# Graph layers on one core: the last stage recast with features on the partitions, node degrees taken in the pattern stage

## The chip, the core and the metric

The kernel runs on one NeuronCore of a Trainium2 chip. Such a core has TensorE (matmuls, with the weight load as its own instruction), VectorE, ScalarE and GpSimd (POOL in the profile), and SyncE (SP), which here only issues DMAs. Each engine executes its own list of instructions in order; semaphores tie them together. The metric is the device time of one execution in microseconds (us); before the change the median of three runs is 4073.85 us (4073.61 to 4083.79).

## The reference

Sixteen graphs of 1024 nodes with 128 features each pass through four layers; every layer is `x = layernorm(x + layer(x, adj))`. `adj` is symmetric in its pattern but not in its values, sparse (some eight neighbours a node), and never negative. Cut to what matters:

```python
# layer 0: attention over the neighbours
x = _layernorm(x + _L0(x, adj, ...))
# layer 1: thin the pattern row by row, then three graph convolutions
adj_d = adj * _dilate(adj > 0)
for l in 1, 2, 3:                      # h0 = x
    deg = clip(sum(adj_d, -1), 1)
    out = (adj_d @ h / deg) @ Wr + h @ Wx + b
    h_l = batchnorm(relu(out / norm(out)))
x = _layernorm(x + concat(h1, h2, h3) @ Wl + bl)
# layer 2
x = _layernorm(x + relu(adj @ (x @ W + b) + x))
# layer 3: A1 = adj + I, d = rsqrt(sum(A1, -1))
x = _layernorm(x + ((A1 * d[:, None] * d[None, :]) @ x) @ B)
```

After the thinning nearly every node keeps no edge but itself; the few others ("slots", at most 128 a graph) are handled apart. A general path, not executed for this data, stands behind a flag.

## The kernel before

The kernel is written for a tile framework: the code gives operations on tiles, and the framework orders each engine's instructions, by their place in the program and by when it reckons them ready, and sets the semaphores. So a queue's order is near the program's, but loads can stand earlier. Four stages follow one another; B is 16 graphs, T is 8 tiles of 128 nodes, N = 1024, F = P = 128.

**phase_att** (layer 0) is not touched. It leaves x1 in DRAM in two forms, `x1_d` (nodes by features) and `x1T_d` (features by nodes), and the 0/1 pattern `mask_d` in f16.

**phase_pattern** (layer 1's thinning) has a generator `find(b)` for each graph. It loads the 2 MB pattern `m` (L599, SP; three buffers), counts each row with eight ScalarE activations with a sum (L603), builds `md` on GpSimd (L607), settles which nodes are small with matmuls against `m` (L617, L621), numbers the remaining ones as slots (L644, L646), gathers their adjacency rows by an indirect DMA on GpSimd's queue (L664), multiplies the pattern with the slots' one-hot matrix (L673, after which `m` is free), turns the gathered rows with TensorE (L703), copies them with ScalarE (`turned`, L705) and multiplies again (L709). `rolling(tasks, depth, lag)` interleaves the generators: at most three graphs are open, and a graph is begun once the one before has made four steps. `settle` and `alone` finish the pattern.

**phase_conv** (the three convolutions) runs over 18 sets a layer: 16 graphs and two sets of slots. For a graph it takes `hT` (features by nodes; in layer 1 loaded from `x1T_d`, L914, later made from `uT` by batch norm's scale and shift, L910), multiplies it on GpSimd with a broadcast row `dd` (load L944, product L946), makes `pq` with 16 matmuls (L949, L950), adds the bias (L952), norms and rectifies to `u` (L954 to L964) and turns `u` into the SBUF tile `uT` one set later (`turn`, L896 to L901). In layers 2 and 3 each `hT` is written to `hT_d` (L912). At the end the slots' share of the output goes to `os_d` (L1009).

**phase_end** (the projection of layer 1, layers 2 and 3, three layer norms) works on one graph at a time, nodes on the partitions. `start(b)` loads the 4 MB transposed adjacency (`adj`, L1058, two buffers), x1 and the h's, and per tile of 128 nodes does four matmuls with h as the stationary side (L1081, L1082), adds, and takes row statistics; `layernorm_tail` (L65 to L69) computes 1/std with a GpSimd power (L67) and scales with eight VectorE operations. `layer2` turns x with TensorE (`turned`, L1048, L1049), makes `vals` = x W + b with a 129th column of ones (L1095, L1096), and for each of eight node tiles sums eight matmuls with a 128x128 piece of the adjacency stationary and 129 columns of `vals` moving (L1102); the extra column comes out as the node's degree (L1106), from which `d` follows (L1114). `layer3` does the same with `v3` = d (x W3) and 128 columns (L1123 to L1138) and writes y (L1140, L1141). The order in the program is

```python
    start(0)
    for b in range(B):
        layer2(b)
        if b + 1 < B:
            start(b + 1)
        layer3(b)
```

Of the kernel before, what the change touches and what calls it, by code (L numbers as in the profile page):

```python
# [10 lines left out]
F32 = mybir.dt.float32  # L11
# [11 lines left out]
P = 128  # L23
# [527 lines left out]
def phase_pattern(ctx, tc, t, c, mask_d, dd_d, slots_d, keep, flags):  # L551
# [44 lines left out]
    def find(b):  # L596
# [7 lines left out]
        yield  # L604
        md = wp.tile([P, T, P], F16, name="md", bufs=3)
        for ti in range(T):
            nc.gpsimd.tensor_tensor(md[:, ti, :], m[:, ti, ti * P : (ti + 1) * P], less, ALU.mult)  # L607
        s = sm.tile([P, T], F16, name="s")
# [16 lines left out]


# [6 lines left out]
        nc.vector.tensor_tensor(left[:, b, :], deg, pu, ALU.subtract)  # L633

# [16 lines left out]
        yield  # L651
        pc = ps_s.tile([P, P + 1], F32, name="pc", tag="ps")
# [15 lines left out]
        yield  # L668

# [17 lines left out]
        yield  # L687
        pr = ps_s.tile([P, P + 1], F32, name="pr", tag="ps")
# [8 lines left out]
        yield  # L697

# [7 lines left out]
        yield  # L706
        pv = ps_s.tile([P, P], F32, name="pv", tag="ps")
# [155 lines left out]
def phase_conv(ctx, tc, t, c, x1_d, x1T_d, dd_d, slots_d, keep, hT_d, uT, os_d):  # L863
# [17 lines left out]
    wl = cp.tile([P, 3, F], F32, name="wl")  # L881
    nc.sync.dma_start(wl, t["L1_gnn_Wl"].rearrange("(l p) f -> p l f", p=P))

    for layer in (1, 2, 3):
# [7 lines left out]
        def turn(s, u):  # L892
            for half in range(2):
# [6 lines left out]
                nc.scalar.copy(to, flat)  # L900
                nc.vector.bn_stats(stats[:, 2 * s + half, :], flat)  # L901

        late = None
        for s in range(SETS):
# [3 lines left out]
            if layer > 1:  # L908
                src = uS[:, layer - 2, (s - B) * N : (s - B + 1) * N] if slots else uT[:, s * N : (s + 1) * N]
                nc.scalar.activation(hT, src, AF.Identity, scale=bn[:, 0:1], bias=bn[:, 1:2])  # L910
                if not slots:
                    nc.sync.dma_start(hT_d[layer - 2][s], hT)  # L912
# [100 lines left out]
def phase_end(ctx, tc, t, c, x1_d, keep, hT_d, uT, os_d, ys, out):  # L1013
# [3 lines left out]
    ap = ctx.enter_context(tc.tile_pool(name="e_a", bufs=2))  # L1017
    wp = ctx.enter_context(tc.tile_pool(name="e_w", bufs=2))
    small = ctx.enter_context(tc.tile_pool(name="e_s", bufs=4))
    ps_p = ctx.enter_context(tc.tile_pool(name="e_pp", bufs=2, space=PSUM))  # L1020
    ps_g = ctx.enter_context(tc.tile_pool(name="e_pg", bufs=4, space=PSUM))
    ps_t = ctx.enter_context(tc.tile_pool(name="e_pt", bufs=2, space=PSUM))

    bn = keep.bn[2]
    node_row = cp.tile([P, N], F16, name="node_row")
    nc.sync.dma_start(node_row, t["q_node_row"])
    wl = cp.tile([P, 3, F], F32, name="wl")
    nc.sync.dma_start(wl, t["L1_gnn_Wl"].rearrange("(l p) f -> p l f", p=P))
    bl = cp.tile([P, F], F32, name="bl")
    nc.sync.dma_start(bl, row_broadcast(t["L1_gnn_bl"], F))  # L1030
# [6 lines left out]
    vals = []  # L1037
    for i in range(2):
        v = cp.tile([P, T, F + 1], F32, name=f"vals{i}")
        nc.vector.memset(v[:, :, F : F + 1], 1.0)  # L1040
        vals.append(v)

    def turned(x):
        xT = wp.tile([P, N], F32, name="xT")
        for half in range(2):
            pt = ps_t.tile([P, 4, P], F32, name="pt")
            for j in range(4):
                nc.tensor.transpose(pt[:, j, :], x[:, half * 4 + j, :], c.ident)  # L1048
            nc.scalar.copy(xT[:, half * 512 : half * 512 + 512], pt.rearrange("p t i -> p (t i)"))  # L1049
        return xT  # L1050

    S = {}

    def start(b):

        s = S[b] = Consts()
        s.adj = ap.tile([P, T, N], F32, name="adj")
        nc.sync.dma_start(s.adj, t["adjT"][b].rearrange("(t p) i -> p t i", p=P))  # L1058
        s.x = wp.tile([P, T, F], F32, name="x")
        nc.sync.dma_start(s.x, x1_d[b].rearrange("(t p) f -> p t f", p=P))  # L1060
        h = []
        for l in range(3):
            hT = wp.tile([P, N], F32, name=f"h{l}")
            if l < 2:
                nc.sync.dma_start(hT, hT_d[l][b])  # L1065
            else:
                nc.gpsimd.tensor_scalar(
                    hT, uT[:, b * N : (b + 1) * N], bn[:, 0:1], bn[:, 1:2], op0=ALU.mult, op1=ALU.add
                )
            h.append(hT)  # L1070

        to = wp.tile([P, N], F32, name="to", bufs=1)
        nc.gpsimd.tensor_scalar(to, node_row, keep.node[:, b : b + 1], None, op0=ALU.is_equal)
        end = wp.tile([P, F], F32, name="end")
        nc.sync.dma_start(end, os_d[:, b, :])
        mv = small.tile([P, T, 2], F32, name="mv")
        for it in range(T):
            at = slice(it * P, (it + 1) * P)
            pp = ps_p.tile([P, F], F32, name="pp")
            for l in range(3):  # L1080
                nc.tensor.matmul(pp, h[l][:, at], wl[:, l, :], start=l == 0, stop=False)  # L1081
            nc.tensor.matmul(pp, to[:, at], end, start=False, stop=True)  # L1082
            o = small.tile([P, F], F32, name="o", bufs=2)
            nc.vector.tensor_tensor(o, pp, bl, ALU.add)  # L1084
            nc.vector.tensor_tensor(s.x[:, it, :], o, s.x[:, it, :], ALU.add)  # L1085
            row_stats(nc, small, s.x[:, it, :], mv[:, it, :])
        layernorm_tail(nc, small, c, s.x, mv, s.x)

    def layer2(b):
        s = S[b]  # L1090
        xT = turned(s.x)
        v = vals[b % 2]
        for it in range(T):
            pp = ps_p.tile([P, F], F32, name="pp")
            nc.tensor.matmul(pp, xT[:, it * P : (it + 1) * P], w2, start=True, stop=True)  # L1095
# [737 lines left out]
```

## Time and profile before

| what | value | from |
|---|---|---|
| runs | 4083.79, 4073.85, 4073.61 us | the times |
| profiled execution | 4084.57 us, its span 4082.8 us | the profiled run |
| mean granted TensorE clock | 0.892 | the profiled run |
| phase_att | to about 2265 us | first load of the pattern stage |
| find() of the pattern stage | 2273 to 2640 us | L599 to L710 |
| settle, alone | 2640 to 2727 us | L750 to L849 |
| phase_conv | 2727 to 3226 us | L949 to L1009 |
| phase_end | 3226 to 4082.8 us | L1058 to the last output |
| L1102, layer 2's matmuls | 2048 instructions of 275 ns (median) | group by line |
| L1129, layer 3's matmuls | 2048 instructions of 275 ns (median) | group by line |
| DMA over the span | 341.32 MB, 84 GB/s | the page |

An f32 matmul of the program is two matmul instructions with a weight load each, here called passes, so that 1024 matmuls of L1102 are 2048 instructions. The duration of one is not its cost: matmuls overlap, and the distance between the starts counts. "Busy" is the share of time in which an engine has an instruction under way. "PEld" is TensorE's weight load, which runs beside the matmuls. The clock is what was granted to TensorE, as a part of full speed.

### The profile page before, as it was taken

The numbers are of one execution on the slowest core, as the hardware profiler recorded it, in microseconds if no ns is written. First come the engines' busy times: TensorE is split into PE (matmuls) and PEld (weight loads), VectorE is DVE, ScalarE is ACT, GpSimd is POOL, SyncE is SP. The second block draws the span as 40 slices with busy tenths as digits, with TensorE's granted clock in tenths as the row PEclk, the third lists the DMA queues.
The fourth block names the chain that finished last, engine by engine and source line by source line (L and its number), as shares of the span: only waits on it lengthen the run. The fifth ranks groups of instructions, "written<-read, shape, count | busy, mean of one in ns | idle before, by whom it ended". The sixth has DMA issues, their size and how long they took to land. (4 is left out here: it accounts for less than half of the span.)

```text
span 4082.8 us, 81190 instructions
## 1 busy us (share of the span) xinstructions
PE 3260.5 (80%) x30587; PEld 2820.9 (69%) x30587; DVE 2887.1 (71%) x10905; ACT 1216.5 (30%) x3329; POOL 1633.7 (40%) x2069
## 2 busy tenths in 40 slices
PE   4888888888888888888999565666667599999997
PEld 2776766676666666676777465646666588888887
DVE  3788888888878888788899445576556366666665
ACT  3433333333333333333333453302334200000000
POOL 9545554545454445545432221125546222222221
PEclk9999999999989999999999676778778799999999
DMA  5222122212212221222100342223323323333331
GB/s 144 80 65 68 47 66 71 65 48 68 65 55 57 70 65 48 65 68 65 33 22 12 132 151 88 70 88 118 116 80 127 143 104 125 125 124 125 124 113 41
DMA packets 146435, 341.32 MB, mean 84 GB/s; under 512 B 12848, under 2 KB 52272, under 8 KB 145904
## 3 DMA queue, kind: packets, MB, share of 16 engines
q1 hardware_dynamic: 135536, 301.41, 23.4%
q0 software_dynamic: 10496, 34.62, 2.5%
q8 instruction: 242, 3.96, 0.4%
q14 instruction: 161, 1.32, 0.1%
HBM read 258.32 MB, written 77.66 MB: 82 GB/s over the span
## 5 line engine op out<-in xcount | busy, mean ns | idle before, releaser
L384 PE MATMUL pg<-ch,oh 104*128 104x256 bf16 x4800 | 908.6, 286 | 120.9 <-ACT hg L395 116.8
L420 PE MATMUL pa<-hg,we 128*104 128x129 f32 x3200 | 672.4, 303 | 106.7 <-DVE we L417 99.0
L420 PEld LDWEIGHTS pa<-hg,we 128*104 128x104 f32 x3200 | 462.0, 179 | 264.2 <-DVE we L417 167.6
L386 PE MATMUL pg<-a,oh 104*128 104x128 bf16 x4800 | 590.0, 227 | 0.0
L417 DVE TENSOR_SCALAR we<-k_id,idc,e 128x104 f32<-128x104 f16 x1600 | 588.6, 386 | 0.0
L384 PEld LDWEIGHTS <-oh 104*128 104x128 bf16 x4800 | 430.1, 102 | 174.5 <-issue 125.6
L391 DVE SCALAR_TENSOR_TENSOR junk<-pg,w_a 128x128 f32<-128x128 f32 x1600 | 409.4, 285 | 166.8 <-PE pg L386 133.6
L234 POOL TENSOR_SCALAR mask<-ld 104x1024 f16<-104x1024 f32 x144 | 400.7, 2782 | 312.1 <-DVE one_way L336 170.8
L386 PEld LDWEIGHTS <-oh 104*128 104x128 bf16 x4800 | 427.2, 102 | 52.0
L395 ACT COPY hg<-pg 128x256 f32<-128x256 f32 x800 | 293.9, 372 | 405.9 <-DVE junk L391 396.2
L1102 PE MATMUL pg<-vals,adj 128*128 128x129 f32 x2048 | 262.1, 285 | 0.0
L237 ACT ACTIVATE neg<-ld 104x1024 bf16<-104x1024 f32 x144 | 152.2, 1057 | 348.5 <-DMA ld<-in_adjT 348.5
L1102 PEld LDWEIGHTS pg<-vals,adj 128*128 128x128 f32 x2048 | 255.2, 203 | 0.0
L1129 PE MATMUL pg<-v,adj 128*128 128x128 f32 x2048 | 240.2, 276 | 0.0
L1129 PEld LDWEIGHTS pg<-v,adj 128*128 128x128 f32 x2048 | 235.0, 192 | 0.0
L1049 ACT COPY xT<-pt 128x512 f32<-128x512 f32 x64 | 36.0, 587 | 657.0 <-PE pt L1048 657.0
L349 ACT CAST oh<-pw 104x512 bf16<-104x512 f32 (+3 forms) x288 | 138.0, 485 | 214.2 <-PE pw L346 213.6
L387 PE MATMUL ids<-k_id_col,oh 104*128 104x1 f16 x1600 | 179.4, 167 | 25.7 <-ACT idc L403 25.7
L311 DVE TENSOR_TENSOR g<-k_slot,off 105x1280 f16<-105x1280 f16 (+9 forms) x160 | 159.1, 994 | 52.1 <-ACT off L307 51.6
L949 PE MATMUL pq<-w,hT 128*128 128x128 f32 x768 | 168.1, 305 | 17.9 <-ACT hT L910 11.7
L285 PE MATMUL pw<-w_all,xT 128*104 128x512 f32 x320 | 182.2, 653 | 0.0
L964 DVE SCALAR_TENSOR_TENSOR u<-q,nrm 128x1024 f32<-128x1024 f32 x54 | 89.4, 1655 | 121.8 <-POOL nrm L962 121.8
(310 smaller groups left out, 7193.7 us busy)
## 6 DMA issues: line engine op xcount, KB each, us to landing
adj<-in_adjT SPq DMA_DIRECT2D x16, 4096.0 KB
ld<-in_adjT SPq DMA_DIRECT2D x144, 416.0 KB
m<-mask_d SPq DMA_DIRECT2D x16, 2048.0 KB
mask_d<-mask SPq DMA_DIRECT2D x144, 208.0 KB
dd<-dd_d SPq DMA_DIRECT2D x48, 512.0 KB
hT_d<-hT SPq DMA_DIRECT2D x32, 512.0 KB
h<-hT_d SPq DMA_DIRECT2D x32, 512.0 KB
xT<-in_xTp SPq DMA_DIRECT2D x16, 520.0 KB
```

The lines of the kernel that those rows point to most:

```text
L234: nc.gpsimd.tensor_scalar(mt[:W, s, :N], ld[:W], 0.0, None, op0=ALU.is_gt)
L285: nc.tensor.matmul(pw[:W], d.xT[:, i * W : (i + 1) * W], w_all, start=True, stop=True)
L384: nc.tensor.matmul(pg[:, n, :], other, d.ch[:W, j, p, :], start=p == 0, stop=False)
L386: nc.tensor.matmul(pg[:, n, :F], own, a3[:W, p, :], start=False, stop=p == 2)
L387: nc.tensor.matmul(ids[:, j : j + 1], own, k_id_col[:W], start=True, stop=True)
L391: nc.vector.scalar_tensor_tensor(junk, pg[:, n, :F], 0.0, w_a2, op0=ALU.max, op1=ALU.mult, accum_out=d.sc[:, at : at + 1],)
L395: nc.scalar.copy(hg[:, j0 : j0 + 2, :F], pg[:, :, F:])
L417: nc.vector.tensor_scalar(we[:, j, :], k_id, idc[:, j : j + 1], e[:, j : j + 1], op0=ALU.is_equal, op1=ALU.mult)
L420: nc.tensor.matmul(pa[:W], we[:, j, :], hg[:, j, :], start=j == 0, stop=j == NG - 1)
L949: nc.tensor.matmul(pq[:, it, :], hT[:, at], w[:, :F], start=True, stop=False)
L1102: nc.tensor.matmul(pg, s.adj[:, jt, it * P : (it + 1) * P], v[:, jt, :], start=jt == 0, stop=jt == T - 1)
L1129: nc.tensor.matmul(pg[:, :F], s.adj[:, jt, it * P : (it + 1) * P], v[:, jt, :], start=jt == 0, stop=jt == T - 1,)
```

## The change

The diff has three parts.

1. *Degrees in the pattern stage.* `find(b)` gets a helper `weights(ti)`: it loads 128 rows of the adjacency in f32 (512 KB, SP, four buffers) and sums them with a ScalarE activation into `keep.deg`. Its eight calls are spread over the steps of `find`. The column of ones in `vals` goes.
2. *phase_conv writes u instead of h.* `turn` writes each half of `uT` to `u_d` (three layers, two writes of 256 KB a graph); the writes of `hT_d` go. `uT` becomes a tile of this stage. The columns' means are taken out of `Wl`, so that layer 1's output needs no mean in its layer norm.
3. *phase_end is rewritten* as a generator `batch(b)` for each graph, two of them interleaved by `rolling(..., 2, 6)`; `adj` has three buffers. Batch norm is folded into `wl` and a constant; d for all graphs is computed at the start with 16 GpSimd powers. The projection and layer 2 run with features on the partitions: `wl` or `v2` stationary, 512 columns of u or of the adjacency moving. Layer norm 1 takes the variance with one-column matmuls against 1/F (`pv`) and spreads 1/std over the partitions with matmuls against the identity (`pr`). The result of layer 2 is turned to nodes on the partitions with TensorE (`pt`), and layer 3 then works as before with 128x128 pieces of the adjacency stationary. Scaling of layer norms 2 and 3 moves from VectorE to ScalarE.

```diff
             junk = wp.tile([P, N], BF16, name="junk")
             nc.scalar.activation(junk, m[:, ti, :], AF.Relu, accum_out=deg[:, ti : ti + 1])
         yield
+
+        def weights(ti):
+
+            a = wp.tile([P, N], F32, name="a_rows", bufs=4)
+            nc.sync.dma_start(a, t["adj"][b, ti * P : (ti + 1) * P, :])
+            junk = wp.tile([P, N], BF16, name="junk")
+            nc.scalar.activation(junk, a, AF.Relu, accum_out=keep.deg[:, b, ti : ti + 1])
+
         md = wp.tile([P, T, P], F16, name="md", bufs=3)
         for ti in range(T):
             nc.gpsimd.tensor_tensor(md[:, ti, :], m[:, ti, ti * P : (ti + 1) * P], less, ALU.mult)
+        weights(0)
         s = sm.tile([P, T], F16, name="s")
         nc.vector.tensor_scalar(s, deg, KEEP - 1.0, None, op0=ALU.is_le)
         yield
@@ -623,6 +632,7 @@
                 )
             return pu
...
+        weights(1)
...
-    wl = cp.tile([P, 3, F], F32, name="wl")
+    uT = cp.tile([P, B * N], F32, name="uT")
+    wl = keep.wl
     nc.sync.dma_start(wl, t["L1_gnn_Wl"].rearrange("(l p) f -> p l f", p=P))
+    mean = small.tile([P, 3], F32, name="mean_w")
+    nc.vector.tensor_reduce(mean, wl, AX.X, ALU.add)
+    nc.vector.tensor_scalar(mean, mean, 1.0 / F, None, op0=ALU.mult)
+    nc.vector.tensor_tensor(wl, wl, mean.unsqueeze(2).to_broadcast([P, 3, F]), ALU.subtract)
 
     for layer in (1, 2, 3):
...
                 nc.scalar.copy(to, flat)
+                if s < B:
+                    nc.sync.dma_start(u_d[layer - 1][s, :, half * 512 : half * 512 + 512], to)
                 nc.vector.bn_stats(stats[:, 2 * s + half, :], flat)
...
                 nc.scalar.activation(hT, src, AF.Identity, scale=bn[:, 0:1], bias=bn[:, 1:2])
-                if not slots:
-                    nc.sync.dma_start(hT_d[layer - 2][s], hT)
...
-def phase_end(ctx, tc, t, c, x1_d, keep, hT_d, uT, os_d, ys, out):
+def phase_end(ctx, tc, t, c, x1T_d, keep, u_d, os_d, ys, out):
...
+    share = cp.tile([P, P], F32, name="share")
+    nc.vector.memset(share, 1.0 / F)
+
+    pm = ps_s.tile([P, 4, P], F32, name="pm", tag="ps")
+    nc.tensor.matmul(pm[:, 0, :], share, w3, start=True, stop=True)
+    nc.vector.tensor_tensor(w3, w3, pm[:, 0, :], ALU.subtract)
+
...
+    for l in range(3):
+        nc.tensor.matmul(
+            pm[:, 1, :], keep.bn[l][:, 1:2].to_broadcast([P, P]), keep.wl[:, l, :],
+            start=l == 0, stop=l == 2,
+        )
+        nc.vector.tensor_scalar(wl[:, l, :], keep.wl[:, l, :], keep.bn[l][:, 0:1], None, op0=ALU.mult)
+    nc.vector.tensor_tensor(bl, bl, pm[:, 1, :], ALU.add)
+    nc.tensor.transpose(pm[:, 2, :], bl, c.ident)
+    const = cp.tile([P, 1], F32, name="const")
+    nc.vector.tensor_copy(const, pm[:, 2, 0:1])
+
+    d_all = cp.tile([P, B, T], F32, name="d_all")
+    nc.gpsimd.tensor_scalar(d_all, keep.deg, 1.0, None, op0=ALU.add)
+    for b in range(B):
+        nc.gpsimd.tensor_tensor(d_all[:, b, :], d_all[:, b, :], c.mhalf, ALU.pow)
+
+    def big(name):
+        return ps_b.tile([P, N], F32, name=name, tag="pb")
...
+    def norm(tiles, mv, name):
+
+        for it, z in enumerate(tiles):
+            row_stats(nc, small, z, mv[:, it, :])
+        ve = small.tile([P, T], F32, name=f"ve_{name}")
+        nc.gpsimd.tensor_tensor(ve, mv[:, :, 1], c.eps, ALU.add)
+        rs = small.tile([P, T], F32, name=f"rs_{name}")
+        nc.gpsimd.tensor_tensor(rs, ve, c.mhalf, ALU.pow)
+        off = small.tile([P, T], F32, name=f"off_{name}")
+        nc.vector.scalar_tensor_tensor(off, mv[:, :, 0], -1.0, rs, op0=ALU.mult, op1=ALU.mult)
+        return rs, off
...
+    def batch(b):
+        adj = ap.tile([P, T, N], F32, name="adj")
+        nc.sync.dma_start(adj, t["adjT"][b].rearrange("(t p) i -> p t i", p=P))
+        x = wide("x1")
+        nc.sync.dma_start(x, x1T_d[b])
+        u = []
+        for l in range(3):
+            w = wide(f"u{l}")
+            nc.sync.dma_start(w, u_d[l][b])
+            u.append(w)
+        end = wp.tile([P, F], F32, name="end")
+        nc.sync.dma_start(end, os_d[:, b, :])
+
+        to = wide("to")
+        nc.gpsimd.tensor_scalar(to, node_row, keep.node[:, b : b + 1], None, op0=ALU.is_equal)
+        yield
+
+        pz = big("pz")
+        for l in range(4):
+            for h in (slice(0, 512), slice(512, N)):
+                nc.tensor.matmul(
+                    pz[:, h], wl[:, l, :] if l < 3 else end, u[l][:, h] if l < 3 else to[:, h],
+                    start=l == 0, stop=l == 3,
+                )
+        z = wide("z1")
+        nc.vector.scalar_tensor_tensor(z, pz, const, x, op0=ALU.add, op1=ALU.add)
+        sq = wp.tile([P, N], F32, name="sq", tag="to")
+        nc.scalar.activation(sq, z, AF.Square)
+        yield
+        pv = ps_s.tile([P, 4, P], F32, name="pv", tag="ps")
+        for it in range(T):
+            nc.tensor.matmul(
+                pv[:, 0, it : it + 1], sq[:, it * P : (it + 1) * P], share[:, 0:1], start=True, stop=True
+            )
+        ve = small.tile([P, T], F32, name="ve")
+        nc.vector.tensor_scalar(ve, pv[:, 0, :T], LN_EPS, None, op0=ALU.add)
+        rs = small.tile([P, T], F32, name="rs")
+        nc.gpsimd.tensor_tensor(rs, ve, c.mhalf, ALU.pow)
+        yield
+        pr = big("pr")
+        for it in range(T):
+            nc.tensor.matmul(
+                pr[:, it * P : (it + 1) * P], rs[:, it : it + 1].to_broadcast([P, P]), c.ident,
+                start=True, stop=True,
+            )
+        x2 = wide("x2")
+        nc.vector.tensor_tensor(x2, z, pr, ALU.mult)
+        yield
+
+        v = rows("v2")
+        for k, ph in enumerate(halves("ph")):
+            for j in range(4):
+                at = (k * 4 + j) * P
+                nc.tensor.matmul(ph[:, j, :], x2[:, at : at + P], w2, start=True, stop=True)
+            nc.vector.tensor_tensor(
+                v[:, k * 4 : k * 4 + 4, :], ph, b2.unsqueeze(1).to_broadcast([P, 4, F]), ALU.add
+            )
+        yield
+        pg = big("pg")
+        for m in range(T):
+            for h in (slice(0, 512), slice(512, N)):
+                nc.tensor.matmul(pg[:, h], v[:, m, :], adj[:, m, h], start=m == 0, stop=m == T - 1)
+            if m == 3:
+                yield
+        z2 = wide("z2")
+        nc.vector.tensor_tensor(z2, pg, x2, ALU.add)
+        nc.vector.scalar_tensor_tensor(z2, z2, 0.0, x2, op0=ALU.max, op1=ALU.add)
+        yield
+        pt = halves("pt")
+        for it in range(T):
+            nc.tensor.transpose(pt[it // 4][:, it % 4, :], z2[:, it * P : (it + 1) * P], c.ident)
+        mv = small.tile([P, T, 2], F32, name="mv2")
+        rs, off = norm([pt[it // 4][:, it % 4, :] for it in range(T)], mv, "2")
+        d = d_all[:, b, :]
+        scale = small.tile([P, T], F32, name="scale")
+        nc.gpsimd.tensor_tensor(scale, rs, d, ALU.mult)
+        x3 = rows("x3")
+        for it in range(T):
+            nc.scalar.activation(
+                x3[:, it, :], pt[it // 4][:, it % 4, :], AF.Identity,
+                scale=rs[:, it : it + 1], bias=off[:, it : it + 1],
+            )
+        yield
+
+        v = rows("v3")
+        for k, pw in enumerate(halves("pw")):
+            for j in range(4):
+                it = k * 4 + j
+                nc.tensor.matmul(pw[:, j, :], z2[:, it * P : (it + 1) * P], w3, start=True, stop=True)
+                nc.scalar.activation(v[:, it, :], pw[:, j, :], AF.Copy, scale=scale[:, it : it + 1])
+        yield
+        mv = small.tile([P, T, 2], F32, name="mv3")
+        for k in range(2):
+            pg = ps_s.tile([P, 4, P], F32, name="pg3", tag="ps")
+            for j in range(4):
+                it = k * 4 + j
+                for m in range(T):
+                    nc.tensor.matmul(
+                        pg[:, j, :], adj[:, m, it * P : (it + 1) * P], v[:, m, :],
+                        start=m == 0, stop=m == T - 1,
+                    )
+                if j == 1:
+                    yield
+            o = small.tile([P, 4, F], F32, name="o", bufs=1)
+            nc.vector.tensor_tensor(o, pg, v[:, k * 4 : k * 4 + 4, :], ALU.add)
+            for j in range(4):
+                it = k * 4 + j
+                nc.vector.scalar_tensor_tensor(
+                    x3[:, it, :], o[:, j, :], d[:, it : it + 1], x3[:, it, :], op0=ALU.mult, op1=ALU.add
+                )
+            yield
+        rs, off = norm([x3[:, it, :] for it in range(T)], mv, "3")
+        y = ys[b % 2]
+        for it in range(T):
+            nc.scalar.activation(
+                y[:, it, :], x3[:, it, :], AF.Identity, scale=rs[:, it : it + 1], bias=off[:, it : it + 1]
+            )
+        nc.gpsimd.dma_start(out[b].rearrange("(t p) f -> p t f", p=P), y)
+        yield
+
+    rolling([(b, batch(b), []) for b in range(B)], 2, 6)
...
+        keep.deg = lp.tile([P, B, T], F32, name="keep_deg")
+        keep.wl = lp.tile([P, 3, F], F32, name="keep_wl")
         ys = [lp.tile([P, T, F], F32, name=f"y{i}") for i in range(2)]
```

## The prediction

> **What bounds the kernel now.** I read the page first, then busy time by stretch, then the chain of waits and the timeline of one batch, and last the two queues that get new work (ScalarE's and SP's).
>
> ```profile
> span 4082.8 us, 81190 instructions
> PE 3260.5 (80%) x30587; PEld 2820.9 (69%) x30587; DVE 2887.1 (71%) x10905; ACT 1216.5 (30%) x3329; POOL 1633.7 (40%) x2069
> ```
>
> The attention stage, which the change leaves alone, ends at about 2265 us. The other stages, cut at their first and last instructions (columns: stretch, length, busy time of five engines, granted clock, DMA share, GB/s):
>
> ```profile
> core 0: us, PE busy (x) PEld busy (x) DVE busy (x) ACT busy (x) POOL busy (x), PEclk, DMA share, GB/s
> 2273.00:2640.00 367.00, 223.97 (x3652) 215.44 (x3652) 166.00 (x428) 174.88 (x337) 74.83 (x144) 0.71 0.34 118
> 2727.00:3226.00 499.00, 340.85 (x2368) 326.14 (x2368) 288.71 (x299) 174.35 (x221) 247.81 (x225) 0.81 0.33 106
> 3226.00:3268.00 42.00, 17.08 (x100) 16.13 (x101) 11.89 (x47) 1.17 (x2) 11.09 (x7) 0.60 0.84 312
> 3268.00:4046.00 778.00, 709.15 (x5635) 679.90 (x5634) 502.31 (x2076) 74.85 (x180) 177.08 (x147) 0.94 0.32 115
> ```
>
> The rows are find(), phase_conv, the end stage's first loads, and its steady part. Find is bound by no engine: none is over 61% busy. The steady end stage is TensorE's: 91% busy. The chain of waits gives its period, 51.2 us a batch, as the distance of these two rows:
>
> ```profile
> 3514.18 1.66 POOL rstd L67
> ...
> 3565.39 1.66 POOL rstd L67
> ```
>
> The timeline says what one batch spends. Each f32 matmul is two passes.
>
> ```profile
> 3499.77 12.72 PE L1129 MATMUL pg<-v,adj 128*128 128x128 f32 x112
> 3518.26 0.49 PE L1095 MATMUL pp<-w,xT 128*128 128x128 f32 x2 [2.35 <-DVE vals L1096]
> 3520.03 0.64 PE L1095 MATMUL pp<-w,xT 128*128 128x128 f32 x2
> 3539.03 2.27 PE L1048 MATMUL pt<-ident,x 128*128 128x128 f32 x8 [1.65 <-DVE x L69]
> 1000.33 1.08 PE L285 MATMUL pw<-w_all,xT 128*104 128x512 f32 x2
> ```
>
> 112 passes of 128 columns in 12.72 us, the last lasting 0.28: 0.112 us a pass. A batch has 64 (L1081, L1082), 16 transposes, 16, 128, 16 and 128 passes: 368 x 0.112 = 41.2 us. The other 10 us are stalls (2.35 and 1.65 us above) and the half-rate passes after them (a pair starts every 0.43 us at 3520, twice the 0.22 of a full-speed pair). The last row, from the attention stage, prices a 512-column pass: two take 1.08 us and one lasts 0.653 (L285's mean), so they start 0.427 us apart.
>
> **The change, part by part: the end stage.** Moving 512 columns streams the same columns through the array. Four narrow passes cost 4 x 0.112 = 0.448 us, one wide pass 0.427. Layer 2's aggregation goes from 128 passes (14.3 us) to 32 (13.7); the head projection from 64 (7.2) to 16 (6.8). Layer 3's aggregation keeps the adjacency stationary, 128 narrow passes, 14.3: the label does not hold there. Of 16 transposes 8 stay (0.9). New are pr (16 passes, 1.8) and pv (16 one-column passes; not shown in f32, between the 0.03 of L617's f16 rows and 0.112: 0.5 to 1.8, I take 1.8). ph and pw stay at 1.8 each. Sum 6.8 + 1.8 + 1.8 + 1.8 + 13.7 + 0.9 + 1.8 + 14.3 = 42.9 us against 41.2. So TensorE gets no less work; only the 10 lost us can be won.
>
> [...]
>
> What can be lost again: in a batch, between the end of pg and a full-rate pg3, lie z2 (two 128x1024 VectorE operations, 1.22 each as at L952 and L964, with hand-overs 2.8), the first transposes 0.5, eight pairs of statistics at 0.45 (3.6), ve, rs and scale on POOL (0.2 + 1.65 + 0.2, with hand-overs 2.75), eight x3 and eight v3 on ScalarE at 0.31 (L1124's rate, 5.0), less 1.8 in which pg3's first passes already run: 12.9 us. TensorE can fill it with pt 0.9, pw 1.8 and the next batch's pz 6.8, maybe its pv: idle 1.5 to 3.4, and a half-rate stretch after it (3 us at half rate, 1.7 lost, as after the two stalls above). The next batch's waits for z, rs, x2 and v2 (about 10 us) are covered by pg3's 14.3. Period: 12.9 + 14.3 + 1.8 + 1.8 + 13.7 + 1.7 = 46.2, I take 46.5 for hand-overs. Ends: 42.9, no stall at all, and 42.9 + 10 = 52.9, the losses stay.
>
> [...]
>
> VectorE falls to about 18 us a batch (nine 1024-wide or two-half operations, 16 statistics pairs, 8 of 0.35), from 32 of 51; ScalarE rises from 5 to 10; neither binds. The degree column's L1106 and L1114 vanish, off the path except 1.65 us of POOL.
>
> Head: 16 pow of d_all at 1.65 us (L1114's) are queued on POOL ahead of the first `to` (2.9). From 3222.6, where the stage's tiles come free, POOL reaches the end of `to` at 3252. The loads (6.1 instead of 5.6 MB at the 312 GB/s shown) end near 3246 and hide behind it. The rest of pz at half rate, z, sq, pv, rs, pr, x2, ph, v2 add 18: pg starts at 3270.6 and ends at 3285, where L1102 ended at 3281. Tail: after the last pg no next batch fills the gap: 12.9 + 1.3 + 1.7 cold + 14.3 + 4.2 (o, x3, statistics) + 5.2 (rs, y) + 6.2 (out, as now) = 45.8, now 36.1. End: 3285 + 15 x 46.5 + 45.8 = 4028, that is **-54.5 us**; by the two ends 3974 (-109) and 4124 (+42).
>
> **The pattern stage.** Per batch eight 512 KB loads on SP's queue and eight row sums on ScalarE. The price of one sum is L603's: 128 activations in 133.5 us, 1.04 each.
>
> ```profile
> L603 ACT ACTIVATE junk<-m 128x1024 bf16<-128x1024 f16 x128 | 133.5, 1052 | 18.5 <-DMA m<-mask_d 18.5
> L705 ACT COPY turned<-pt 128x1024 f32<-128x1024 f32 x16 | 16.2, 1012 | 100.7 <-PE pt L703 55.0 <-PE pu L642 45.8
> L703 PE MATMUL pt<-ident,rows 128*128 128x128 f32 x128 | 30.8, 413 | 63.9 <-DMA rows<-in_adj,keep_index 63.9
> ```
>
> So +133 us on a ScalarE that is idle 192 of 367. Between 0, all of it in those waits, and +133, none. In the waits it costs nothing itself, since ScalarE stands before L705 for TensorE; without that cover it is the full 133. But 64 MB more also move. Three mask loads of 2 MB landed 5.3 to 5.6 us apart (380 GB/s), so one new load is 1.35 us, all 172 us beside the 110 now used. TensorE stands for the gathered rows at L703, 63.9 us; sharing the engines with one new load each adds 16 x 1.35 = 22. A mask load finds up to four new loads ahead on SP's queue (0 to 5.4 us; two, 2.7, taken); three batches are in flight, so 16 x 2.7 / 3 = 14. Four short ScalarE steps a batch meet a running row sum one time in three, half of 1.04: 4. Taken: **+40 us**; it is nearer the low end because the rows show long waits to fill.
>
> **phase_conv.** 96 writes of 256 KB replace 32 of 512 KB. In layer 1 they are new on SP, ahead of later x1T_d and dd_d loads, each behind turn()'s copies; in layers 2 and 3 they replace a write behind hT's activation. DMA is at a third. 0, between -10 (hT comes free sooner) and +12 (layer 1 waits 0.8 us for each of 16 loads). The three operations on Wl's means are under 2 us, hidden behind the first loads.
>
> **Sum.** -54.5 + 40 + 0 = -14.5. The profiled execution took 4084.6 (span 4082.8, 1.8 around it), 10.7 above the median of 4073.85; its stages are taken to scale alike. Forecast: 4073.85 - 14.5 = **4059 us**.
>
> **Rivals.** R1, slower: SP issues in order, and its queue now couples the mask loads to ScalarE.
>
> ```profile
> SPq L599 <- PE pg L673: 235.9, 13, 25.6
> ```
>
> SP stands at the mask load for 236 us in all. New loads queued ahead of it wait for one of four a_rows buffers, which ScalarE frees, and ScalarE stands 6.3 us a batch before L705. If each mask load takes over one such stand, the stage pays 16 x 6.3 = 101: -54.5 + 101 = +46, **4120**. It decides once the pattern stage costs more than 67. For it: loads behind loads. Against: four buffers, and TensorE ends most waits. R2, slower too: pt and pw hold all four small PSUM banks, pv cannot start, the gap stays empty; period 50, end stage -2, with +40: **4112**. R3, faster: pz and pv fill the gap without a dip (44.5: -84) and the row sums hide (+10): **4000**. For it: VectorE's load falls, and it ended both stalls shown.
>
> **How the numbers follow.** Forecast 36% (own range 4034 to 4086), R1 27%, R2 12%, R3 21%, the rest 4%. 0.3% is 12 us, about what a measurement of this kernel tells from no change. Half of the forecast's case and R3 are faster: 0.42; most of its other half is the same: 0.17; R1, R2 and the remainder slower: 0.41. The range, 3985 to 4135, takes in R1, R2 and R3 and leaves out the ends above.
>
> **What will show it.** Layer 2's wide passes 0.427 apart; a period of 46 to 47 with one idle of 2 to 3 us after pg; POOL's 16 pow at the end stage's start; find 30 to 50 us longer with SP waiting longer at L599; phase_conv within 12 of 499. A period under 45 or over 48, or find under 10 or over 70 longer, makes the prediction wrong.

## The result, and the profile after

The changed kernel takes 4166.48 us (median of 4 runs, 4162.85 to 4171.17); the kernel before, on the same chip, 4076.39. The ratio is 1.0219, 95% interval 1.0201 to 1.0237: **slower by 2.2%**. The forecast was 4059, its range ended at 4135. The profiled execution took 4171.17 us.

The head of its page; columns as before:

```profile
span 4169.4 us, 76952 instructions
PE 3285.0 (79%) x28676; PEld 2674.9 (64%) x28676; DVE 2596.5 (62%) x9556; ACT 1425.9 (34%) x3793; POOL 1612.9 (39%) x2054
```

VectorE lost 291 us of work and ScalarE gained 209; TensorE's busy time hardly moved. Busy time by stretch (find(), phase_conv, the end stage's first loads, its steady part; the same columns as in the prediction):

```profile
core 0: us, PE busy (x) PEld busy (x) DVE busy (x) ACT busy (x) POOL busy (x), PEclk, DMA share, GB/s
2271.00:2708.00 437.00, 236.06 (x3642) 227.82 (x3643) 166.10 (x424) 308.02 (x593) 72.17 (x144) 0.63 0.70 246
2798.00:3296.00 498.00, 343.64 (x2368) 328.96 (x2368) 286.93 (x301) 174.32 (x221) 248.21 (x226) 0.81 0.35 123
3299.00:3343.00 44.00, 21.54 (x69) 14.98 (x69) 4.35 (x10) 1.06 (x1) 30.70 (x18) 0.62 0.98 381
3343.00:4115.00 772.00, 703.03 (x3711) 512.94 (x3711) 220.32 (x753) 140.88 (x367) 134.94 (x116) 0.93 0.33 121
```

Cut at the stages' own first and last instructions (first L603 to the last copy of V; TensorE's first and last instruction of phase_conv; from there to the end), spans go from 4082.8 to 4169.4 like this:

| stage | before | after | difference | predicted |
|---|---|---|---|---|
| attention (not touched), to the first L603 | 2283 | 2271 | -12 | 0 |
| find() | 354.9 | 436.6 | **+81.7** | +40 |
| settle, alone | 90.9 | 90.2 | -1 | 0 |
| phase_conv | 493.5 | 497.6 | +4 | 0 |
| end stage | 860.3 | 873.6 | **+13.3** | -54.5 |

Attention ended between 2244 and 2283 us in the profiled executions of all kernels that leave it alone. So the stages' own lengths are compared below, and not whole times that differ by less than these 39 us.

**The end stage.** The chain of waits gives its period (columns: start, length, engine, tile, line):

```profile
3459.34 3.43 PE pz L1128 x8
3512.73 3.43 PE pz L1128 x8
3561.72 3.43 PE pz L1128 x8
```

53.4 and 49.0 us in turn, 102.4 for two graphs: exactly the 2 x 51.2 of before. TensorE's timeline after one pg (columns: start, length, instructions; in brackets the idle time ahead and what ended it):

```profile
3547.72 14.00 PE L1169 MATMUL pg<-adj,v 128*128 128x512 f32 x32
3561.56 3.60 PE L1128 MATMUL pz<-u,wl 128*128 128x512 f32 x8
...
3569.30 0.61 PE L1196 MATMUL pw<-w,z 128*128 128x128 f32 x4
3574.14 3.58 PE L1139 MATMUL pv<-share,sq 128*128 128x1 f32 x16 [4.23 <-ACT sq L1135]
3577.57 0.77 PE L1196 MATMUL pw<-w,z 128*128 128x128 f32 x2
3578.14 0.63 PE L1205 MATMUL pg<-v,adj 128*128 128x128 f32 x2
```

The 32 wide passes take 13.84 us, as priced. But TensorE then does two of pw's eight products, stands 4.23 us for the squares, and takes 3.58 us for pv, about double the 1.84 us that pv takes at full clock (at 3536.90 us). The next lines show pw's products one at a time: four of them write into one PSUM tile, and in the program each is followed by the ScalarE step that reads it (L1197), which the next product waits for (12 such waits between 3400 and 3962 us, 11.6 us in all). The squares in turn stand on ScalarE behind the eight x3 steps (L1186), and these wait for VectorE's statistics:

```profile
3570.24 2.90 ACT L1186 ACTIVATE x<-pt,off,rs 128x128 f32<-128x128 f32 x8 [18.16 <-DVE off L1105]
3572.99 1.09 ACT L1135 ACTIVATE sq<-z 128x1024 f32<-128x1024 f32 x1
```

The granted clock of the changed kernel, as busy time by stretch, cut where the clock changes (PEclk is the column after the five engines):

```profile
3568.72:3572.13 3.41, 1.19 (x6) 0.60 (x4) 1.37 (x2) 1.89 (x6) 3.33 (x3) 1.00 0.59 179
3572.13:3575.54 3.41, 1.40 (x7) 1.40 (x7) 0.00 (x0) 2.47 (x6) 0.93 (x1) 0.50 0.47 154
3575.54:3585.78 10.24, 9.73 (x45) 9.43 (x45) 0.17 (x1) 2.21 (x6) 1.66 (x1) 0.50 0.00 1
3585.78:3674.53 88.75, 82.08 (x448) 57.48 (x446) 29.50 (x101) 14.52 (x39) 16.16 (x15) 1.00 0.41 150
```

The same view of the kernel before:

```profile
3464.74:3468.15 3.41, 1.08 (x9) 1.08 (x10) 2.87 (x12) 0.00 (x0) 0.97 (x1) 1.00 1.02 418
3468.15:3471.56 3.41, 3.41 (x18) 3.41 (x17) 1.06 (x4) 0.00 (x0) 0.00 (x0) 0.50 1.04 345
3471.56:3488.63 17.07, 15.42 (x135) 14.88 (x133) 10.55 (x47) 0.00 (x0) 3.46 (x3) 1.00 0.33 117
```

In these rows a window of 3.41 us in which TensorE has little work under way (1.19 us, 1.08 us) is followed by half clock. After: 13.65 us at half clock for two graphs, in one piece. Before: four pieces of 3.41, also 13.65. TensorE's idle time is 9.2 us for two graphs in both. The changed stage moved its stalls and kept their cost.

**The pattern stage.** Groups of ScalarE's instructions in the changed find() (columns: busy time, mean ns, idle time ahead and its releaser):

```profile
L611 ACT ACTIVATE junk<-a_rows 128x1024 bf16<-128x1024 f32 x128 | 134.5, 1055 | 29.2 <-DMA a_rows<-in_adj 28.2
L611 ACT ACTIVATION_READ_ACCUMULATOR junk<-a_rows 128x1 f32 x128 | 24.9, 194 | 0.0
L720 ACT COPY turned<-pt 128x1024 f32<-128x1024 f32 x16 | 16.1, 1004 | 36.6 <-PE pt L718 20.9 <-PE pu L653 15.7
```

The waits there, of SP's queue and of the engines (total us, times, longest):

```profile
SPq L609 <- ACT junk L611: 222.8, 102, 18.7
SPq L599 <- PE pg L686: 53.3, 5, 18.2
...
POOL md L615 <- DMA m<-mask_d: 189.1, 15, 27.5
...
PE pt L718 <- DMA rows<-in_adj,keep_index: 84.4, 16, 13.2
```

Before, SP stood 235.9 us at the mask load itself, which so went out as soon as a buffer was free. Now it stands 222.8 us at row loads (L609) whose buffer ScalarE has not freed, and the mask load behind them is late: GpSimd waits 189 us for `m`, before 121.

### The profile page after: what moved, and what is told of

Read it like the earlier page. It is cut to its first block, busy times and chain, and to the rows that moved or that the text cites. A ratio compares the mean times of both kernels' runs of the same rounds, so it can differ in the third digit from the quotient of the medians.

```text
span 4169.4 us, 76952 instructions
## 1 busy us (share of the span) xinstructions
PE 3285.0 (79%) x28676; PEld 2674.9 (64%) x28676; DVE 2596.5 (62%) x9556; ACT 1425.9 (34%) x3793; POOL 1612.9 (39%) x2054
## 5 line engine op out<-in xcount | busy, mean ns | idle before, releaser
L1205 PE MATMUL pg<-v,adj 128*128 128x128 f32 x2048 | 265.8, 286 | 7.9 <-ACT x L1186 7.6
L1205 PEld LDWEIGHTS pg<-v,adj 128*128 128x128 f32 x2048 | 254.7, 201 | 19.5 <-ACT x L1186 15.6
L1169 PE MATMUL pg<-adj,v 128*128 128x512 f32 x512 | 224.4, 594 | 0.0
L1222 ACT ACTIVATE y<-x,off,rs 128x128 f32<-128x128 f32 x128 | 51.0, 481 | 396.8 <-DVE off L1105 396.8
L970 PE MATMUL pq<-w,hT 128*128 128x128 f32 x768 | 169.6, 307 | 13.2 <-ACT hT L933 11.8
L971 PE MATMUL pq<-w,hd 128*128 128x128 f32 x768 | 167.9, 305 | 8.3 <-DMA slots_w<-slots_d 5.0
```

The costliest lines, as they stand in the source:

```text
L970: nc.tensor.matmul(pq[:, it, :], hT[:, at], w[:, :F], start=True, stop=False)
L1169: nc.tensor.matmul(pg[:, h], v[:, m, :], adj[:, m, h], start=m == 0, stop=m == T - 1)
L1205: nc.tensor.matmul(pg[:, j, :], adj[:, m, it * P : (it + 1) * P], v[:, m, :], start=m == 0, stop=m == T - 1,)
```

## The experiments

Sixteen kernels. "Pair" is the steady time of two graphs in the end stage, taken over ten graphs. Where no ratio is given, a kernel was executed once, and its stage lengths and its one time carry no interval.

**Which stage loses: e1.** `weights()` returns at once, the degrees are set to 7.

> The changed kernel with the row loads and row sums left out of the pattern stage (the degrees are a constant 7, so the output is not the reference's). Theory: the loss lies in the pattern stage, find() is back from 437 to 350-362 us, and the end stage stays at 865-875 us, so the whole is 4075-4095 us, no faster than before. Rival: the new loads also cost the end stage or the convolution, then the end stage falls below 850 too and the whole is under 4065.

Measured: find() 353.9, end stage 870.7, whole 4093.22, ratio 1.0038 (1.0020 to 1.0056). The first theory holds: the pattern stage's loss is the degrees', and the new layers by themselves win nothing.

**What in the degrees costs: e2, e3, e4.**

```diff
 e2   a = wp.tile([P, N], F32, name="a_rows", bufs=4)
      nc.sync.dma_start(a, t["adj"][b, ti * P : (ti + 1) * P, :])
-     nc.scalar.activation(junk, a, AF.Relu, accum_out=...)
 e3  -nc.sync.dma_start(a, ...)
     -nc.scalar.activation(junk, a, AF.Relu, accum_out=...)
     +nc.scalar.activation(junk, still, AF.Relu, accum_out=...)
 e4  -nc.sync.dma_start(a, ...)
     +nc.gpsimd.dma_start(a, ...)
```

> The changed kernel with the row loads kept on SP's queue and the row sums left out (degrees a constant). If ScalarE's time and order make the loss (theory A), find() is 355-375 us; if the DMA traffic and SP's queue make it (theory B), it stays at 420-440 us. In between, both.

> The changed kernel with the row sums kept on ScalarE but taken of one resident tile, and the row loads left out (degrees a constant). Theory A (ScalarE): find() 420-440 us. Theory B (DMA and SP's queue): 360-385 us.

> The changed kernel complete, its row loads issued by GpSimd instead of SP, so that the mask loads and the constants on SP no longer stand behind a row load that waits for its buffer. If the in-order queue of SP makes the loss, find() falls from 437 to 355-395 us; if ScalarE or the bytes themselves make it, it stays at 425-445 us.

Measured find(): 406.3 with the loads alone (+52 against e1), 372.6 with the sums alone (+19), 436.6 with both (+83), 414.9 with the loads on GpSimd's queue. Whole: 4147.33, 4114.04, 4144.96. What SP's queue waits for in e2's find():

```profile
SPq L610 <- DMA a_rows<-in_adj: 186.3, 90, 9.6
```

In e3's:

```profile
SPq L601 <- PE pg L686: 233.4, 13, 22.1
```

And in e4's:

```profile
SPq L599 <- PE pg L686: 273.9, 13, 26.2
```

So 159 us of ScalarE work (134.5 + 24.9) cost 19 by themselves: most of it does fill waits, as the prediction took it to. The loads by themselves cost 52, even where nobody reads them, and both together 83, which is 12 more than the two parts. By its own bounds e2's 406.3 lies between theory A and theory B, and e3's 372.6 is B's: ScalarE alone does not make the loss, and the loads make the larger part of it.

How the loads cost 52 in e2 was not followed to the end. SP stands 186 us there at row loads, for the four buffers' earlier transfers, and the mask loads stand behind; but GpSimd waits only 24.3 us for `m` (before 121, after 189), so late masks are not what e2 shows.

Taking the loads off SP's queue (e4) brings SP back to the mask load, GpSimd's wait for `m` down to 50.2 us, and find() down by 22, to 414.9, which lies between the ranges of its two theories and not at e3's 372.6. The loads still cost 42 there: 64 MB more move, and GpSimd's queue, which also issues the gathers of `rows`, now stands 169.6 us for ScalarE to free an `a_rows` buffer; these two were not told apart. So SP's order is 22 of the 83 us.

**What holds the end stage: e5, e6, e7.**

```diff
 e5   for j in range(4):
          it = k * 4 + j
          nc.tensor.matmul(pw[:, j, :], z2[:, it * P : (it + 1) * P], w3, ...)
+     for j in range(4):
+         it = k * 4 + j
          nc.scalar.activation(v[:, it, :], pw[:, j, :], AF.Copy, ...)
 e6  -nc.scalar.activation(sq, z, AF.Square)
     +nc.vector.tensor_tensor(sq, z, z, ALU.mult)
```

> The changed kernel with layer 3's eight small products issued ahead of the ScalarE steps that read them (four products, then four steps), so that they no longer go one by one through one bank. Theory S (the stalls after the wide product set the period): the pair of batches falls from 102.4 us to 97-100. Theory G (the period is tied to the grid of 3.413 us windows on which the clock changes): it is 102.4, 98.99 or 95.57, and nothing between. If the period is PE's own work, 102.4 stays.

> The changed kernel with the squares of L1135 made by VectorE right behind z instead of by ScalarE behind eight x3 steps. Theory S: pv starts some 4 us earlier in every second batch, the 4.23 us idle of PE is gone, the clock no longer halves there (4 slow windows of 30 in a pair become 0 to 2), pair of batches 95-99 us, end stage 870 to 815-850. Rival (the chain through pw and v3 is as long): 102.4 stays.

> The changed kernel with both: products first, squares on VectorE. Theory S: pair of batches 90-96 us, no slow window in the steady state, end stage 760-820 us (the predicted period of 46.5 would be 93.0 a pair). Theory G: a multiple of 3.413 us as long as any slow window is left in the pair, free of it when none is. Rival: no better than the better of the two alone.

Measured: pair 98.95 (e5), 102.41 (e6), 94.2 (e7); end stage 846.5, 869.1, 806.1; whole 4148.73, 4156.48, 4099.73. TensorE's timeline at the gap, in e5:

```profile
3572.22 1.95 PE L1139 MATMUL pv<-share,sq 128*128 128x1 f32 x16 [2.89 <-ACT sq L1135]
```

In e6:

```profile
3560.24 1.22 PE L1196 MATMUL pw<-w,z 128*128 128x128 f32 x4 [3.54 <-ACT v L1197]
3561.26 3.41 PE L1139 MATMUL pv<-share,sq 128*128 128x1 f32 x16
```

In e7:

```profile
3552.15 1.92 PE L1139 MATMUL pv<-share,sq 128*128 128x1 f32 x16 [1.86 <-DVE sq L1135]
```

With the squares early alone (e6), TensorE has pw's third product ahead of pv in its order, and that product waits 3.54 us for v3: one stall steps into the other's place, and e6's theory falls. Taken out together they shorten the pair by 8.2 us, more than the 3.4 and 0 of each alone. Half clock falls from 13.65 to 4.78 us a pair (theory S said none), idle time from 9.2 to 4.9. (e5's 98.95 fits both of its theories; theory G is taken up below.) Between the ends of its first and its last pg, 15 graphs apart, e7 has a period of 46.84 us; the prediction said 46.5.

**Clock or wait: e8, e9.**

```diff
 pv = ps_s.tile([P, 4, P], F32, name="pv", tag="ps")
+for _ in range(10):            # e9: 3
+    nc.tensor.matmul(pv[:, 1:4, :], c.ident, x[:, :384], start=True, stop=True)
```

> The changed kernel with ten products of 128x384 that nobody reads ahead of pv in each batch: 10 x 0.32 = 3.2 us more work for PE at full clock, placed where it otherwise waits for the squares. If the loss is the clock that falls after an idle window, there are fewer slow windows and the pair of batches is 95-102.4 us in spite of the added 6.4 us of work; if it is the wait itself, 103-109 us.

> The changed kernel with three products of 128x384 that nobody reads ahead of pv in each batch, 3 x 0.32 = 0.96 us of PE at full clock, 1.9 us a pair (up to 3.8 at half clock). Theory G (the period locks on the 3.413 us windows of the clock): the pair stays at 102.4 us, or jumps by one whole window to 105.8. Rival (the chain simply adds): 104.3 to 106.2 and not on the grid.

Measured: pair 108.31 with 2.73 us at half clock (e8), 102.85 with 7.51 (e9); whole 4213.35 and 4168.21. The filler of one graph on TensorE's timeline in e8:

```profile
3543.71 6.62 PE L1139 MATMUL pv<-x,ident 128*128 128x384 f32 x20
```

Ten f32 products are 20 passes, and these start 0.32 us apart. So the filler adds 6.4 us a graph and 12.9 a pair, and e9's three products 3.9 a pair: twice what both expectations counted, which took 0.32 us for a product. In e8 the clock was nearly saved, which wins 5.5 us back (half of the 10.9 us that are no longer at half clock), and TensorE's idle time fell by 2.9 us a pair; 12.9 less these two is 4.5, the pair grew by 5.9, and 1.4 are not explained. This filler is longer than the gap, and it begins only after 1.88 us of idle time, released by an x3 step (L1188 in e8), so e8 does not say what one of the gap's own length would give. e9's is shorter and shows how well such a stage hides a change: 3.9 us of added work raise the pair by 0.45, since 6.1 us less at half clock give 3.1 back and the idle time falls by 1.6 (1.2 are left over here). Neither filler made the pair shorter; taking the wait out did (e7).

The lock on whole windows (theory G) does not hold strictly: 30.00, 30.00, 28.99 and 30.00 windows of 3.413 us in before, after, e5 and e6, but 30.13 in e9, 31.73 in e8 and 27.60 in e7.

**Another place for the degrees: e10, e11, e12.** e10 puts the same load and sum ahead of each graph's set in phase_conv; e11 sums the rows that attention loads for its masks; e12 is e11 with e7's two edits and the 16 powers made in phase_conv's third layer.

```diff
 e10 +for r in range(k * 8 // 3, (k + 1) * 8 // 3):   # k: set, over the three layers
     +    nc.sync.dma_start(a, t["adj"][r // T, r % T * P : (r % T + 1) * P, :])
     +    nc.scalar.activation(junk, a, AF.Relu, accum_out=keep.deg[:, r // T, ...])
 e11 -nc.sync.dma_start(ld[:n], t["adjT"][b, s * W : s * W + n, :])
     +nc.sync.dma_start(ld[:n], t["adj"][b, s * W : s * W + n, :])
      nc.scalar.activation(junk[:W], ld[:W], AF.Relu, scale=-1.0, accum_out=...)
     +nc.scalar.activation(junk[:W], ld[:W], AF.Relu, accum_out=sums[:W, s : s + 1])
```

> The changed kernel with the same 128 row loads and row sums moved from the pattern stage to the convolution, 2 or 3 of them ahead of each of its 48 sets. Theory: find() is back at 350-362 us, and the convolution, where ScalarE is busy 35% and the DMA engines 35%, takes most of them in its gaps: 500 to 505-535 us; whole 4085-4125 us. Rival (in-order ScalarE makes each sum a delay there too): the convolution becomes 560-640 us, and nothing is won.

> The changed kernel with the row sums taken in the attention stage from the adjacency rows that it loads for its masks anyway (it loads the adjacency in place of its transpose), so that no load is added; the sums go through DRAM to the layout of the nodes. Theory: find() 350-362 us, attention (2263-2283 us to the start of find) longer by 0-25 us, end stage 870; whole 4085-4115 us. Rival (160 more ScalarE steps of some 1 us delay the steps that TensorE waits for there): attention longer by 60-170 us.

> Row sums in the attention stage, the 16 powers of the degrees made during the convolution's third layer, products first and squares on VectorE in the end stage. Theory (the parts are separate): find() 355, head of the end stage shorter by some 20 us, end stage 780-790 us; whole 3990-4025 us, faster than before by 1.2 to 2%. Rival: attention or the convolution gives the gain back, 4060 us or more.

Measured: e10 find() 352.9, but phase_conv 604.8 (+107), whole 4202.82. e11 find() 353.7, but attention to 2414 (after: 2271) and phase_conv 519.3, whole 4253.50. e12 4208.26, ratio 1.0296 (1.0266 to 1.0326), end stage 809.3. All three rivals hold. ScalarE in e10's phase_conv:

```profile
L919 ACT ACTIVATE junk<-a_rows 128x1024 bf16<-128x1024 f32 x126 | 133.1, 1057 | 57.5 <-DMA a_rows<-in_adj 56.3
...
L919 ACT ACTIVATION_READ_ACCUMULATOR junk<-a_rows 128x1 f32 x126 | 24.1, 191 | 0.0
```

133 + 24 of work and 56 of waiting for loads stand in a queue that was busy 35%, and half of that reaches the stage's end; through which of ScalarE's later steps was not taken apart. A share of 35% was no room. In e11 no load was added; which of attention's waits carries its 140 us was not taken apart either. e12's phase_conv is 540.7, another 21 over e11's, with the powers now in it, and its end stage gained nothing from the early powers (809.3, e7 806.1): the stretch of the first loads, where they stood, has its DMA engines at 0.98 in e12 too (3398 to 3442 us, 377 GB/s), so it is the loads that last.

**Degrees from what is already on the chip: e13, e14, e15, e16.** e7's two edits, no rows loaded; instead, in the end stage:

```diff
+total = wp.tile([P, N], F32, name="total", tag="v2")
+nc.vector.tensor_tensor(total, adj[:, 0, :], adj[:, 1, :], ALU.add)   # e14: gpsimd
+for m in range(2, T):
+    nc.vector.tensor_tensor(total, total, adj[:, m, :], ALU.add)
...
+for it in range(T):
+    nc.tensor.matmul(pv[:, 1, it : it + 1], total[:, it * P : (it + 1) * P], share[:, 0:1], ...)
+nc.vector.tensor_scalar(d, pv[:, 1, :T], float(F), 1.0, op0=ALU.mult, op1=ALU.add)
+nc.gpsimd.tensor_tensor(d, d, c.mhalf, ALU.pow)
```

> Products first and squares on VectorE in the end stage as before (e7_both), and the degrees made there too, from the transposed adjacency that the batch holds anyway: VectorE adds its eight tiles into one (7 adds of some 1.2 us by the row of L1173, 8.6 us a batch), and eight one-column products on TensorE sum over the partitions (1.68 us by the row of L1139), read ahead of pv; no load and no ScalarE step is added anywhere. Theory (the new layers are worth having once the degrees cost neither loads nor ScalarE): find() 350-362 us, end stage 806 + 0 to 40 us, whole 4010-4060 us, faster than before. Rival (the adds delay VectorE's own chain from z to v2 and the pair of batches goes back to 102.4 us): 4080 us or more.

> The same, the seven adds on GpSimd, which is busy 17% of this stage against VectorE's 29%. If VectorE's order is what the adds cost, this end stage is shorter than that of e13; if GpSimd's powers (L1103, L1145) come late behind the adds (2 us and more each), it is longer, the pair of batches 98 us or more.

> e13 with the two powers of a batch (degrees, and the norm of layer 1) taken in one GpSimd instruction of 128x16 in place of two of 128x8 (1.65 us each by L1103). Theory: one power off the way from z to x2, up to 1.65 us a batch, 26 us in all if that way sets the period, 0 if it doesn't: whole 4030-4057 us. Rival (the norm now waits for the degrees' sums): 4057-4075 us.

> Products first, squares on VectorE, and no degrees at all (a constant 7, so the output is not the reference's): what the changed layers would give if the degrees were free. Theory: find() 354 and end stage 806, whole 4010-4025 us. Against e13 this prices the degrees made from the resident adjacency.

Measured:

| run | find() | end stage | pair | whole | ratio |
|---|---|---|---|---|---|
| e13 | 355.1 | 846.5 | 99.6 | 4056.85 | 0.9966 (0.9954 to 0.9979) |
| e14 | 356.8 | 890.6 | 105.1 | 4098.35 | one execution |
| e15 | 356.6 | 863.3 | 101.3 | 4076.46 | 1.0017 (1.0006 to 1.0028) |
| e16 | 354.0 | 803.1 | 93.5 | 4001.09 | one execution |

e13 takes the changed kernel's loss back. Its whole time lies 0.34% under that of the kernel before, but the stages behind attention are together only 3.4 us shorter than before's (1796.2 against 1799.6); the rest of the difference between the profiled executions lies in attention, which e13 leaves alone. That e13's stages beat the kernel before is not shown. e16 says what the new layers are worth if the degrees were free: an end stage 57.2 us shorter than before's 860.3. The degrees take 43 of them back in e13. VectorE's adds, by group, and the products that follow them on TensorE:

```profile
L1105 DVE TENSOR_TENSOR total<-total,adj 128x1024 f32<-128x1024 f32 x78 | 95.5, 1224 | 2.2
L1125 PE MATMUL pv<-share,total 128*128 128x1 f32 x208 | 24.6, 248 | 3.2 <-ACT x L1178 3.2
```

The adds are 1.22 us each, seven a graph, as priced, and TensorE is not seen to wait for them. What a pair pays, 99.6 against e16's 93.5, is TensorE's: 32 one-column passes are 3.6 us at 0.112 (pv's 16 take 1.84 us in e7, the last some 0.17), time at half clock rises from 3.41 to 10.24 us, which costs 3.4, and 0.9 less idle time comes off. With the adds on GpSimd it is worse (e14): 2.42 us each, and GpSimd's powers stand behind them in the order. e15's single power is no help: it takes 2.92 us where two took 3.30, the norm now waits for the sums too, and the time lies 1.5 us above even the rival's range.

## Why the prediction was wrong, by its own steps

**Right.** TensorE's work is no smaller: 32 wide passes take 13.84 us, 13.7 said. Head: pg begins 47.8 us after phase_conv's end, predicted 48. Tail after the last pg 43.8, predicted 45.8. phase_conv is 4 us longer, within the 12 allowed; but it is longer in all kernels that share it (e1 to e9 and e13 to e16: 498 to 508 us), so 0 was a little too kind. Most of the sums hides in ScalarE's waits: 19 us are left of 159.

**Right by luck.** The rows' gather waits grew by 20.5 us (63.9 to 84.4), predicted 22. But with the loads alone (e2) they fell to 34.6, with the sums alone (e3) to 24.9, and the stage was still 52 and 19 us longer: these waits move about and do not measure the loss.

**Wrong: the period.** "TensorE can fill it with pt 0.9, pw 1.8 and the next batch's pz 6.8, maybe its pv: idle 1.5 to 3.4, and a half-rate stretch after it (3 us at half rate, 1.7 lost)". The list of work was right, its order was not. pv's squares stand behind eight x3 steps on ScalarE, pw's products go one at a time through a shared tile, and the half-rate stretch is 13.65 us a pair, 6.8 lost, where 1.7 a graph was said. The period stayed at 51.2 where 46.5 was said: 15 x 4.7 = 70 us, against 68 of error in the stage. The mechanism as such holds: with the two waits out the period is 46.6 (e16) and the end stage -57.2, predicted -54.5. A filler of a gap counts only if each piece's own inputs and outputs are free at that time, and in that order; this was not asked of sq, for which TensorE stands 4.23 us, and of pw, for which it stands 3.54 in e6.

**Wrong in size: the pattern stage**, +40 said, +82 measured. Two terms were too small. The loads (22 for the gathers, 14 for the mask loads) were said to cost 36; alone they cost 52 (e2). The mask loads' term ("two, 2.7, taken") counted transfer time ahead of a mask load on SP's queue; what stands ahead is row loads that wait for ScalarE to free a buffer, 222.8 us of standing. That was rival R1, and its mechanism is seen (e4), though not its price: 22 of the 83 us go when the loads leave SP's queue, 42 stay with the loads and 19 with the sums. The sums were said to cost 4 and cost 19 (e3). As written, four steps in each of 16 graphs, one in three delayed by half of 1.04 us, are 11 us; 4 comes out only if that is divided by the three graphs in flight. A sum is also 1.25 us of ScalarE, not 1.04: each is followed by a read of the accumulator of 0.19 us, which had a row of its own. And loads and sums together cost 12 us more than each alone, which no term held.

**The rivals.** R1's 4120 and R2's 4112 each took one loss; both came, so the end lay above the range, which had not joined them. R2 had the place right (the gap after pg) and the cause wrong: what releases pv in the trace is sq, after 4.23 us, and not a PSUM bank. The bank would come next: e8's filler, which writes pv's tile and needs no squares, also stands 1.88 us, until an x3 step has read. No run came to R3's period of 44.5, the period's sum without the 1.7 at half rate: e7, with both waits out, still has 4.78 us a pair at half clock, and e16 3.41. The chances were added a little wrong: half of the forecast's case and R3 are 0.39, not 0.42.

## What to carry to other kernels

In these runs a gap on the bounding engine was filled only by work whose inputs, output banks and place in the order were all free then (pv stood 4.23 us for its squares, in e6 pw 3.54 for v3, in e8 the filler 1.88 for an x3 step): write down for each piece which engine frees it, and what stands ahead on that engine. Two stalls in one gap hid each other (3.4 and 0 us won apart, 8.2 together), so take both out before judging either. And before a new pass over data is put into an idle share of some engine, look for the data where it already lies on the chip: the same degrees cost 83 us in the pattern stage, about 107 in phase_conv, 140 in attention and 43 from the resident tile, where the price is paid on TensorE.

## What the runs showed of the hardware

In the traces of before and after every change of the granted clock lies on one grid of 3.413 us, to within 0.004 us (stretches of 8, 1, 5 and 1 windows in the steady end stage of before, of 26 and 4 in that of after), and the clock is 1.00 or 0.50, nothing else. The graph from 3440.84 us of before has 13 windows at full clock: the two in which TensorE is busy 1.08 and 1.77 us were followed by half clock, the other 11, busy 2.95 us or more, were not. In the two graphs from 3483.38 us of after, one window busy 1.20 us was followed by half clock, and the other 25, busy 1.84 us or more, were not (busy times are cut from modelled ends).

Idle time alone does not decide, though. In e5 TensorE stands 2.89 us for the squares both at 3471.88 and at 3572.22 us, and pv then takes 3.57 us at the one and 1.95 at the other. In e13 half clock follows a window in which TensorE is busy 3.00 of 3.41 us:

```profile
3580.79:3584.20 3.41, 3.00 (x27) 3.00 (x27) 1.39 (x2) 3.41 (x14) 2.44 (x2) 1.00 0.44 163
3584.20:3587.62 3.42, 3.42 (x18) 3.42 (x18) 0.17 (x1) 0.41 (x2) 1.89 (x2) 0.50 0.00 0
```

And the four half-clock windows of the changed kernel run on through a stretch that is busy 9.73 of 10.24 us. No run shows what else decides.

A window at half clock costs up to 1.7 us: in the kernel before, a pair of narrow passes starts every 0.43 us in it (at 3520 us), and every 0.22 at full clock. Stalls and half clock together are why two stages that differ in work, before's and the changed one, show the same 51.2 us a graph (for two graphs 9.2 us idle and 13.65 at half clock in both), and why 3.9 us of added work (e9) lengthened the pair by only 0.45.
